# Joining the last two pairs of a convolution, and which PSUM banks their small products use

## The chip, the cores and the metric

The kernel runs on one core of a Trainium2 chip. The metric is the device time of one execution in microseconds (us). A measurement is the median of several runs.

## What is computed

Each of 64 sequences (batch) with 64 heads of 1024 positions goes through a causal long convolution, whose kernel per head is made from 64 complex exponentials (a state-space model), plus a direct term, under a length mask. The result goes through a mixture of 64 rank-16 experts with the best 16 gated by a softmax, and is added to the input:

```python
kernel = 2.0 * einsum('hn,hnl->hl', Cs, exp(dtA[:, :, None] * arange(L))).real
y = (causal_convolution(u * mask, kernel) + (u * mask) * D) * mask

scores = xf @ Wr.T
top_vals, top_idx = top_k(scores, 16)
G = zeros.at[rows, top_idx].set(softmax(top_vals))
h = einsum('nd,krd->nkr', xf, A)
out = einsum('nkr,kdr->nd', h * G[:, :, None], B) * 2.0
x = x + out
```

All data are fp32.

## The kernel before

The work is done in eight groups g of eight heads, 512 tokens each. A group has a convolution (`conv`), the gates of its tokens (`gates`, `spread_gates`) and the first expert product (`first`, which calls `seven`). After the last group come the second expert products for all groups (`second`), in the second half of the span. Tables of a group's exponentials (`tables`) are made two groups ahead.

A convolution treats its eight heads as four pairs i = 0 to 3, in blocks of 128 positions:

- `into_states(i)` (L618) turns the blocks into states: for each of two parts c, a PSUM tile pu, filled by two products that each use half of the columns of TensorE's array (shape 128*64). ScalarE copies pu to the state tile s (L623).
- `recur` (L366) lets the states decay from block to block, on VectorE, 18 small operations a pair.
- `inside(i)` (L644) opens two PSUM tiles pc, one a head, with a Toeplitz product of the block itself (shape 128*128).
- `across` (L653) adds what the states bring, with 64-row products (shape 64*128), and then multiplies pc by the mask into y on VectorE (L661). `out_of` is `inside` and `across` in one.

PSUM has eight banks, which stand in three pools: `ps_f` (four banks, tag pf) for the products h of the experts (L553), `ps_c` (two, tag pc) for pc, and `ps_k` (two, tag pk) for pu and for all small products: pb and pk in `tables` (transposed columns of the tables, L326, and kernel rows, L293), psh and psc in `gates` (scores, L722 and L731), and pg in `spread_gates` (gates transposed, L766). A tile that is opened in a bank waits until the readers of the tile before it in that bank are done. In convolution 0 alone, pairs 1 and 3 put pc into `ps_f`.

The order of the work: `conv`, `tables` and `first` are Python generators. The main loop advances them in turns: each `yield` of `conv` lets `first` issue one product of 16 matmul instructions, or as many as the yielded number says. `step(n)` inside `conv` advances the tables of a later group by n steps. Steps 1 to 8 make the sines and the tables w; steps 9 to 12 make the four columns of b and their transposes pb; the last ones make pk and the kernel rows. What is issued first is preferred, and a scheduler may then move an instruction that would wait. An fp32 product is two matmul instructions in the trace, a transpose one.

So a convolution from 1 on goes: pairs 0 and 1 into states, `recur(0, 1)`, two of `first`'s products more, pair 0 out and pair 2 in, a product, pair 1 out and pair 3 in, `recur(2, 3)`, a product, table steps, a product, pair 2 out, a product, pair 3 out, table steps. The gates of the group follow at once.

Of the kernel before, what the change touches and what calls it, by code (L numbers as in the profile page):

```python
# [37 lines left out]
F32 = mybir.dt.float32  # L38
# [6 lines left out]
P = 128  # L45
NB = 64
# [17 lines left out]
GP = HG // 2  # L64
NW = P + 1
NCH = NBLK - 1
# [26 lines left out]
def body(ctx: ExitStack, tc, x, xo, lens, par, dvec, at, bm, wt, cst, out):  # L93
# [12 lines left out]
    ps_f = ctx.enter_context(tc.tile_pool(name="ps_f", bufs=4, space=PSUM))  # L106
    ps_c = psum.enter_context(tc.tile_pool(name="ps_c", bufs=2, space=PSUM))
    ps_k = psum.enter_context(tc.tile_pool(name="ps_k", bufs=2, space=PSUM))
# [33 lines left out]
    def load_x(h):  # L142
        t = xp.tile([P, 2, NBLK * NB], F32, tag="x", name=f"x_{h}")
        nc.sync.dma_start(t, x[h : h + 2].rearrange("h p c -> p h c"))
        x_tiles[h] = t
# [57 lines left out]
    def behind_landing(t):  # L203

        tc.keep_in_program_order(G.tensor_copy(landed, t))
# [7 lines left out]
    def fourth_sum(s4, s2):  # L213

        for k in range(0, KH, 2):
            tc.keep_in_program_order(
                G.dma_start(s4[:, k : k + 2, :], at[:, KH + k : KH + k + 2, : L // 2]))
        for k in range(0, KH, 2):
            tc.keep_in_program_order(
                G.dma_start(s4[:, k : k + 2, :], s2[:, k : k + 2, :], accum_op=ALU.add))  # L220
# [144 lines left out]
    def stt(o, a, s, o1, b, o2):  # L365
        V.scalar_tensor_tensor(out=o, in0=a, scalar=s, in1=b, op0=o1, op1=o2)  # L366
        return o
# [157 lines left out]
    def masks():  # L525
        lens_f = prep.tile([P, NB], F32, tag="lensf", name="lens_f")
        V.tensor_copy(lens_f, lens_sb)
        tt(mask, feat.unsqueeze(2).to_broadcast([P, NBLK, NB]),
           lens_f.unsqueeze(1).to_broadcast([P, NBLK, NB]), ALU.is_lt)
# [65 lines left out]
    def conv(g, steps, out):  # L595
        if g == 0:
            next(steps)
        w, bt, turn, toep = tabs.pop(g)
        if g == 0:

            s_more = yp.tile([P, NBLK * TOK], F32, tag="y", name="s_more")
        y = yp.tile([P, NBLK, NS2, HH, NB], F32, tag="y", name=f"y_{g}")
        out.append(y)
        states = {}

        def into_states(i):
            h = g * HG + 2 * i
            if h not in x_tiles:
                load_x(h)
            xt = x_tiles.pop(h)  # L610
            if g == 0 and i == GP - 1:
                s = s_more[:, : 2 * NCH * NB].rearrange("p (c k b) -> p c k b", c=2, b=NB)
            else:
                s = sp.tile([P, 2, NCH, NB], F32, tag="s", name=f"s_{g}_{i}")
            for c in range(2):
                pu = ps_k.tile([P, NCH * NB], F32, tag="pk", name=f"pu_{g}_{i}_{c}")
                for hh in range(2):
                    nc.tensor.matmul(  # L618
                        pu[hh * NS : (hh + 1) * NS, :],
                        lhsT=bt[:, i, (1 - c) * P + hh * NS : (1 - c) * P + (hh + 1) * NS],  # L620
                        rhs=xt[:, hh, : NCH * NB], start=True, stop=True,
                    )
                marks["s"] = nc.scalar.copy(s[:, c], pu.rearrange("p (k b) -> p k b", b=NB))  # L623
            states[i] = xt, s

        def recur(*pairs):
            for k in range(1, NCH):
                for i in pairs:
                    s, a = states[i][1], turn[:, 0, i : i + 1]
                    stt(s[:, :, k, :], s[:, :, k - 1, :], a, ALU.mult, s[:, :, k, :], ALU.add)  # L630
                for i in pairs:
                    s, b = states[i][1], turn[:, 1, i : i + 1]
                    stt(s[:, 0, k, :], s[:, 1, k - 1, :], b, ALU.mult, s[:, 0, k, :], ALU.add)
                for i in pairs:
                    s, nb = states[i][1], turn[:, 2, i : i + 1]
                    stt(s[:, 1, k, :], s[:, 0, k - 1, :], nb, ALU.mult, s[:, 1, k, :], ALU.add)

        def inside(i):
            xt, s = states.pop(i)
            pcs = []  # L640
            for hh in range(2):
                banks, tag = (ps_f, "pf") if g == 0 and i % 2 else (ps_c, "pc")
                pc = banks.tile([P, NBLK * NB], F32, tag=tag, name=f"pc_{g}_{i}_{hh}")
                nc.tensor.matmul(pc, lhsT=toep[:, 2 * i + hh, :], rhs=xt[:, hh, :],  # L644
                                 start=True, stop=False)
                pcs.append(pc)
            return i, s, pcs

        def across(i, s, pcs, pinned=False):
            for c in range(2):  # L650
                for hh in range(2):
                    o = hh * NS
                    m = nc.tensor.matmul(  # L653
                        pcs[hh][:, NB:], lhsT=w[o : o + NS, c, i, 1:],
                        rhs=s[o : o + NS, c].rearrange("p k b -> p (k b)"),
                        start=False, stop=(c == 1),
                    )
                    if pinned:
                        tc.keep_in_program_order(m)
            for hh in range(2):  # L660
                marks["y"] = V.tensor_tensor(  # L661
                    out=y[:, :, i // 2, 2 * (i % 2) + hh, :],
                    in0=pcs[hh].rearrange("p (k b) -> p k b", b=NB), in1=mask, op=ALU.mult)

        def out_of(i):
            across(*inside(i))

        def step(n):
            for _ in range(n):
                next(steps, None)  # L670

        if g == 0:
            step(1)
        into_states(0)
        into_states(1)
        if g == 0:
            step(3)
            masks()
            first_order.close()
            step(1)  # L680
            behind_landing(toep[0:1, HG - 1, 0:1])
            fourth_sum(wa[2], wa[5])
            prep_ctx.close()
        recur(0, 1)
        if g == 0:
            into_states(2)
            into_states(3)
            first_two = inside(0), inside(1)
            across(*first_two[0], True)
            across(*first_two[1])  # L690
            recur(2, 3)
            last_two = inside(2), inside(3)
            yield
            across(*last_two[0], True)
            across(*last_two[1])
            return
        yield
        step(4)
        yield 2

        out_of(0)
        into_states(2)
        yield
        out_of(1)
        into_states(3)
        recur(2, 3)
        yield
        step(5)
        yield
        out_of(2)  # L710
        yield
        out_of(3)
        step(5)


    def gates(g, y):
# [393 lines left out]

    got = []
    steps = conv(0, steps0, got)
    next(steps)
    hp = pool(left, "hp", 1, "left")
# [7 lines left out]
    for g in range(NG):  # L1122
# [29 lines left out]
        for n in conv(g + 1, steps, got):  # L1152
            ahead(products, 1 if n is None else n)
# [40 lines left out]
    for _ in products:  # L1194
# [3 lines left out]
        if n in (5, 6):  # L1198
            i = (1, 6)[n - 5]
# [77 lines left out]
```

## Time and profile before

| | |
|---|---|
| median of three runs | 977.95 us (977.91 to 978.32) |
| the profiled execution | 978.31 us, of which the span that the profile shows is 976.5 us |
| convolution 0 | until about 50 us |
| convolutions 1 to 7 | their first states at 74.9, 137.8, 212.2, about 288.5, 364.8, 441.1 and 517.4 us |
| last score product psh | 564.3 us |
| second expert products | from about 634 us to the end |

Columns of a timeline row: start (us), length (us), engine, line, operation, out<-in, shapes, count. In brackets stands how long the engine was idle just before, and what ended that. PE is TensorE's matmuls, PEld its weight loads, DVE VectorE, ACT ScalarE. The ends of matmuls are modelled, so the distance between two starts says more than a row's length.

### The profile page before, as it was taken

How to read it: one execution, taken by the hardware profiler on the slowest of the kernel's cores; microseconds unless marked ns; L12 is line 12 of the kernel's file. 1: busy time of each engine (PE TensorE's matmuls, PEld its weight loads, DVE VectorE, ACT ScalarE, POOL GpSimd, SP SyncE). 2: the span in 40 equal slices, each digit the busy share in tenths (PEclk: the TensorE clock that was granted, in tenths of full speed). 3: DMA queues.
4: the chain of work that ended last, by engine and by line, in shares of the span. 5: the costliest groups of instructions: out<-in, count | busy, mean ns of one | idle time of the engine just before them, and what ended most of it. 6: DMA issues, size and time to landing. Idle time of an engine off the chain costs nothing.

```text
span 976.5 us, 11964 instructions
## 1 busy us (share of the span) xinstructions
PE 963.7 (99%) x4312; PEld 723.8 (74%) x4312; DVE 724.2 (74%) x1682; ACT 159.7 (16%) x310; POOL 334.8 (34%) x285
## 2 busy tenths in 40 slices
PE   7999999999999999999999999999999999999998
PEld 2476666676676686586676678888888888888887
DVE  8889798597687687686656769778966785686674
ACT  5344151230330221131101000000000000000000
POOL 0212112042023023132123112247545663754555
PEclk9999999999999999999999999999999999999999
DMA  7825234325325305315305254683674466267422
GB/s 281 226 56 167 70 119 141 108 89 155 109 75 159 114 36 158 139 55 157 140 23 167 77 178 162 198 300 105 216 260 132 168 209 231 90 214 266 134 108 108
DMA packets 67456, 143.99 MB, mean 147 GB/s; under 512 B 9478, under 2 KB 18246, under 8 KB 67398
## 3 DMA queue, kind: packets, MB, share of 16 engines
q1 hardware_dynamic: 49378, 94.40, 28.7%
q0 software_dynamic: 16864, 47.22, 15.1%
q10 hardware_dynamic: 1156, 1.61, 0.6%
q8 instruction: 34, 0.56, 0.2%
q14 instruction: 24, 0.20, 0.1%
HBM read 94.89 MB, written 47.25 MB: 146 GB/s over the span
## 4 chain that ended last, share of the span: by engine, by line
PE 93%; DVE 4%; DMA 1%; ACT 1%; issue 0%; POOL 0%; DVEq 0%
PE h L553 39%; PE s L1042 34%; PE pc L644 5%; PE pc L653 5%; PE pu L618 5%; PE psh L722 3%; PE pb L326 1%; PE pk L293 1%; DMA toep<-krows 1%; DMA krows<-ks 0%; PE last L1042 0%; PE pg L766 0%; DVE s L366 0%; PE psc L731 0%; DVE hg L355 0%
## 5 line engine op out<-in xcount | busy, mean ns | idle before, releaser
L366 DVE SCALAR_TENSOR_TENSOR s<-s,turn 128x128 f32<-128x128 f32 (+1 forms) x558 | 153.2, 321 | 26.5 <-ACT s L623 20.2
L553 PE MATMUL h<-y,waa 128*128 128x256 f32 x512 | 120.7, 383 | 0.0
L553 PE MATMUL h<-y,was 128*128 128x256 f32 x512 | 117.6, 381 | 0.0
L553 PE MATMUL h<-ty,was 128*128 128x256 f32 x512 | 116.8, 380 | 0.0
L553 PEld LDWEIGHTS h<-y,waa 128*128 128x128 f32 x512 | 94.4, 190 | 27.1 <-issue 15.3
L553 PEld LDWEIGHTS h<-y,was 128*128 128x128 f32 x512 | 96.0, 190 | 20.9 <-issue 7.2
L553 PEld LDWEIGHTS h<-ty,was 128*128 128x128 f32 x512 | 96.5, 190 | 17.5 <-issue 4.8
L804 POOL TENSOR_TENSOR hg<-h_p,gx 128x512 f32<-128x512 f32 x16 | 28.7, 1796 | 213.3 <-DVE h_p L366 210.3
L804 POOL TENSOR_TENSOR hg<-h_u,gx 128x512 f32<-128x512 f32 x32 | 48.9, 1528 | 112.1 <-DVE h_u L355 111.6
L661 DVE TENSOR_TENSOR y<-pc,mask 128x512 f32<-128x512 f32 x64 | 41.2, 684 | 44.1 <-PE pc L653 44.1
L1056 ACT COPY p<-s 128x512 f32<-128x512 f32 x28 | 16.4, 586 | 312.4 <-PE s L1042 312.4
L901 POOL TENSOR_TENSOR o<-o,acc_a 128x512 f32<-128x512 f32 x32 | 47.7, 1510 | 41.4 <-ACT acc_a L919 21.6
L644 PE MATMUL pc<-x,toep 128*128 128x512 f32 x128 | 60.0, 593 | 0.3 <-DMA toep<-krows 0.3
L553 PE MATMUL h<-ty,waa 128*128 128x256 f32 x256 | 58.6, 381 | 0.0
L777 POOL DMA_DIRECT2D gx<-gt_dram x56 | 33.6, 629 | 67.3 <-DMA gt_dram<-gt 67.3
L623 ACT COPY s<-pu 128x448 f32<-128x448 f32 x62 | 32.9, 532 | 144.3 <-PE pu L618 144.0
L618 PE MATMUL pu<-x,bt 128*64 128x448 f32 x256 | 55.1, 552 | 1.2 <-ACT gt L768 1.2
L553 PEld LDWEIGHTS h<-ty,waa 128*128 128x128 f32 x256 | 48.0, 190 | 9.9 <-issue 3.5
L653 PE MATMUL pc<-s,w 64*128 64x448 f32 x248 | 54.7, 561 | 0.0
L901 POOL TENSOR_TENSOR o<-o,b_room 128x512 f32<-128x512 f32 x32 | 49.2, 1557 | 9.8 <-DVE b_room L355 9.8
L355 DVE TENSOR_TENSOR o<-o,s 128x512 f32<-128x512 f32 x50 | 34.1, 682 | 23.0 <-PE s L1042 17.3
L355 DVE TENSOR_TENSOR hg<-hg 128x512 f32<-128x512 f32 x64 | 43.0, 684 | 9.5 <-POOL hg L804 8.8
(236 smaller groups left out, 1586.5 us busy)
## 6 DMA issues: line engine op xcount, KB each, us to landing
x<-in_x SPq DMA_DIRECT2D x32, 512.0 KB
hg_dram<-hg POOLq DMA_DIRECT2D x16, 1024.0 KB, 5.2
o<-in_xo SPq DMA_DIRECT2D x64, 256.0 KB
out<-o SPq DMA_DIRECT2D x63, 256.0 KB
gx<-gt_dram POOLq DMA_DIRECT2D x56, 256.0 KB, 6.1
qy<-hg_dram SPq DMA_DIRECT2D x28, 512.0 KB
r<-hg_dram SPq DMA_DIRECT2D x26, 512.0 KB
hg_dram<-hg POOLq DMA_DIRECT2D x16, 768.0 KB, 4.4
```

The costliest lines, as they stand in the source:

```text
L355: V.tensor_tensor(out=o, in0=a, in1=b, op=o_)
L366: V.scalar_tensor_tensor(out=o, in0=a, scalar=s, in1=b, op0=o1, op1=o2)
L553: nc.tensor.matmul(bank[:, ii, :], lhsT=fac[n - 1][:, k, (j + ii) * P : (j + ii + 1) * P], rhs=rf[n - 1][:, k, :], start=(first and ii == ...
L618: nc.tensor.matmul(pu[hh * NS : (hh + 1) * NS, :], lhsT=bt[:, i, (1 - c) * P + hh * NS : (1 - c) * P + (hh + 1) * NS], rhs=xt[:, hh, : NCH ...
L623: marks["s"] = nc.scalar.copy(s[:, c], pu.rearrange("p (k b) -> p k b", b=NB))
L644: nc.tensor.matmul(pc, lhsT=toep[:, 2 * i + hh, :], rhs=xt[:, hh, :], start=True, stop=False)
L653: m = nc.tensor.matmul(pcs[hh][:, NB:], lhsT=w[o : o + NS, c, i, 1:], rhs=s[o : o + NS, c].rearrange("p k b -> p (k b)"), start=False, sto ...
L661: marks["y"] = V.tensor_tensor(out=y[:, :, i // 2, 2 * (i % 2) + hh, :], in0=pcs[hh].rearrange("p (k b) -> p k b", b=NB), in1=mask, op=ALU ...
L777: i = queue.dma_start(gx[:, ii, :], gt_dram[g, c * n : (c + 1) * n, :].unsqueeze(1).to_broadcast([n, RANK, TOK]),)
L804: G.tensor_tensor(out=o, in0=a, in1=b, op=op)
L901: tc.keep_in_program_order(G.tensor_tensor(out=o, in0=a, in1=b, op=op_))
L1042: nc.tensor.matmul(bank[:, ii, :], lhsT=left_[i - 1][:, k, ii * P : (ii + 1) * P], rhs=right_[i - 1][:, k, :], start=(first and ii == rows ...
```

## The change

Three edits, all in `conv`, for the groups from 1 on; convolution 0 is as it was.

Pair 1's states pu are opened in the two banks of `ps_c`, not in `ps_k`, so that the states of pairs 0 and 1 have four banks together. Pair 3's tiles pc are opened in the two banks of `ps_k`, not in `ps_c`, so that pairs 2 and 3 can be open at once. And the end of the convolution is written as one stretch: `inside(2)`, `inside(3)`, then `across` for both, with both of `first`'s products ahead of it. The table steps are cut 4, 4 and 6 in place of 4, 5 and 5: none of the transposes pb is issued before the stretch.

```diff
             for c in range(2):
-                pu = ps_k.tile([P, NCH * NB], F32, tag="pk", name=f"pu_{g}_{i}_{c}")
+
+                banks, tag = (ps_c, "pc") if g and i == 1 else (ps_k, "pk")
+                pu = banks.tile([P, NCH * NB], F32, tag=tag, name=f"pu_{g}_{i}_{c}")
...
-                banks, tag = (ps_f, "pf") if g == 0 and i % 2 else (ps_c, "pc")
+                if g == 0:
+                    banks, tag = ((ps_c, "pc"), (ps_f, "pf"))[i % 2]
+                else:
+                    banks, tag = (ps_k, "pk") if i == GP - 1 else (ps_c, "pc")
...
         yield
-        step(5)
-        yield
-        out_of(2)
-        yield
-        out_of(3)
-        step(5)
+        step(4)
+        yield
+        yield
+        last_two = inside(2), inside(3)
+        across(*last_two[0])
+        across(*last_two[1])
+        step(6)
```

## The prediction

> **What bounds the kernel.** I read the page's engine row first, then TensorE's (PE's) timeline, where the start of one row minus the start of the row above is the time that a block really takes (the ends are modelled).
>
> ```profile
> PE 963.7 (99%) x4312; PEld 723.8 (74%) x4312; DVE 724.2 (74%) x1682; ACT 159.7 (16%) x310; POOL 334.8 (34%) x285
> ```
>
> PE is the bound all the way, at a granted clock of 1.00. So only two things can move the time: PE's own blocks becoming shorter, and PE idling. One steady convolution, conv 3, on PE:
>
> ```profile
> 212.20 1.72 PE L618 MATMUL pu<-x,bt 128*64 128x448 f32 x8
> 213.85 0.70 PE L553 MATMUL h<-y,waa 128*128 128x256 f32 x2
> 214.48 1.72 PE L618 MATMUL pu<-x,bt 128*64 128x448 f32 x8
> 216.13 3.29 PE L553 MATMUL h<-y,waa 128*128 128x256 f32 x14
> ...
> 243.62 0.38 PE L326 MATMUL pb<-cst_sb,b 128*128 128x128 f32 x2
> 243.84 3.62 PE L553 MATMUL h<-y,waa 128*128 128x256 f32 x16
> 247.29 1.88 PE L644 MATMUL pc<-x,toep 128*128 128x512 f32 x4
> 249.10 1.77 PE L653 MATMUL pc<-s,w 64*128 64x448 f32 x8
> 250.81 3.72 PE L553 MATMUL h<-ty,was 128*128 128x256 f32 x16
> 254.37 1.88 PE L644 MATMUL pc<-x,toep 128*128 128x512 f32 x4
> 256.18 1.77 PE L653 MATMUL pc<-s,w 64*128 64x448 f32 x8
> 257.88 0.88 PE L326 MATMUL pb<-cst_sb,b 128*128 128x128 f32 x6
> 258.60 0.60 PE L553 MATMUL h<-y,waa 128*128 128x256 f32 x2
> 259.12 1.02 PE L293 MATMUL pk<-b,cst_sb 128*2 128x256 f32 x4
> 260.08 3.65 PE L722 MATMUL psh<-y,wt_sb 128*64 128x512 f32 x16
> ```
>
> No row here idles. But blocks cost more beside a change of tile shape (the column 128*128, 64*128, 128*64). Sixteen h take 3.45 us after pb (243.84 to 247.29) and 3.56 after the 64-row products (250.81 to 254.37): 0.216 each, plus 0.10. Four Toeplitz products (pc, L644) should take 4 x 0.432 = 1.73 at the h's rate and take 1.81. Eight 64-row products (L653) run two at a time, 4 x 0.378 = 1.51, and take 1.70. So an excursion into the 64-row shape costs 0.08 + 0.19 + 0.10 = 0.37, and one into the 128*64 shape (the states' pu: 1.65 for 1.51 of work; two h between, 0.63 for 0.43) 0.34.
>
> That a joint stretch pays once is seen in conv 0, whose last two pairs already run so (chain of waits, then VectorE's timeline):
>
> ```profile
> 44.29 3.21 PE pc L653 x16
> ```
> ```profile
> 46.03 1.29 DVE L661 TENSOR_TENSOR y<-pc,mask 128x512 f32<-128x512 f32 x2 [3.24 <-PE pc L653]
> 47.53 1.29 DVE L661 TENSOR_TENSOR y<-pc,mask 128x512 f32<-128x512 f32 x2 [0.21 <-PE pc L653]
> ```
>
> Sixteen take 3.21, not 2 x 1.70. The stretch starts at 44.22 and the next block at 47.43. The first pair's multiplies start 1.80 after the stretch's start, well inside it, and the second pair's 0.10 after its end. Two multiplies take 1.29, one 0.69.
>
> **The rule on the shapes.** The Trainium skill (TensorEngine Tiling (Array Packing), Tiling Modes) says that a change of tiling mode drains TensorE; it gives no size. If a drain is the 0.10 seen after the 64-row block, two excursions fewer per conv, four changes, give 0.4 us. The rows give 0.37 + 0.34 = 0.7, because entering costs more than leaving. I use the rows.
>
> **Part A, pair 1's states in the out-of-states banks.** In the changed program's order PE issues all sixteen pu on end; the two h between them go elsewhere at 0.43. Before: 212.20 to 216.13, 3.93. After: 3.02 of work + 0.14 = 3.16, or 3.27 as the sixteen pu of conv 1 took in PE's timeline (74.92 to 78.19, with waits for copies). Gain 0.23 to 0.34; I take 0.30, and five convs (3 to 7): **1.5 us**. The banks are free: their earlier readers are multiplies some 20 us back. VectorE's recurrences start from the same copies and have about 4 us until the first product that reads them (end 223.2, product 228.0).
>
> **Part B, the tails of convs 2 to 6.** Let T be the end of the last 64-row product. Before, from the first pb to T, 243.62 to 257.88: 14.26. After: two h blocks 6.91, eight Toeplitz products 8 x 0.432 + 0.08 = 3.54, sixteen 64-row products 3.21: 13.66. Gain 0.60, part of which is only pb moved behind T.
>
> After T, pair 3's sums lie in the small products' banks, which pb needs. That is the new wait. By the conv 0 rows the four multiplies start at T - 1.41, -0.81, +0.10 and +0.70; the third ends at T + 0.79, the fourth at T + 1.39. The changed order is: two h (0.43 + 0.10, until T + 0.53), four pb (waiting for the third multiply), four pb (waiting for the fourth), two h, pk, psh. What a release costs is seen at two places:
>
> ```profile
> 562.81 1.13 PE L553 MATMUL h<-y,waa 128*128 128x256 f32 x4
> 562.91 1.29 DVE L661 TENSOR_TENSOR y<-pc,mask 128x512 f32<-128x512 f32 x2 [2.65 <-PE pc L653]
> ...
> 564.26 0.20 PEld L722 LDWEIGHTS psh<-y,wt_sb 128*64 128x64 f32 x4 [0.72 <-DVE y L661]
> ```
> ```profile
> 25.79 0.20 PEld L326 LDWEIGHTS pb<-cst_sb,b 128*128 128x128 f32 x2 [0.50 <-ACT s L623]
> ```
>
> The multiply's end at 564.20 lets PE go at 564.26. And pb's weight load waits too: at 25.79 load and product start together. The Trainium skill (TensorE: Matmul & The Clock Gate, Part 2) says that the queue pulls weight loads ahead of running matmuls; by that a load would be done when the bank comes free. The row says it isn't: 0.10 more per wait, some 1.2 us over six convs. I take the row. So the first four pb start at T + 0.87 (0.34 idle) and end at T + 1.41; the second four start at T + 1.46 and end at T + 2.00; h 0.53, pk 0.96: psh starts at T + 3.48. Before, 257.88 to 260.08 is 2.20. After holds two h more (0.43), so 3.05 compares: 0.85 lost, 0.60 won, **0.25 us lost** per conv, 1.25 in five. With the load hidden it is 0.14, with a release of 0.15 as before conv 1's psh 0.33: 0.7 to 1.65.
>
> Queued behind pb on PE are pk and psh. psh needs all four multiplies anyway, over by then. ScalarE's copies of pb, VectorE's k (waits for pk) and the sine tables come 1.3 us later after T; they have slack, since the gates' product pg comes over 20 us later in these convs. DMAs, SyncE's and POOL's orders are unchanged.
>
> **Part C, conv 7.** No tables, so no pb behind T. Before, 545.22 to 562.81 is 17.59; after, 3 x 3.45 + 0.10 + 3.54 + 3.21 = 17.21. psh waits for the same multiplies as above. Gain **0.4 us**.
>
> **Part D, conv 1's tail and the seam to conv 2**, where before PE stands:
>
> ```profile
> 123.21 3.65 PE L722 MATMUL psh<-y,wt_sb 128*64 128x512 f32 x16 [0.58 <-DVE y L661]
> ...
> 137.27 0.60 PE L766 MATMUL pg<-cst_sb,sa 128*64 128x128 f32 x4
> ...
> 140.56 0.97 PE L618 MATMUL pu<-x,bt 128*64 128x448 f32 x4 [1.16 <-ACT gt L768]
> ```
>
> Before, from T = 120.36 to the h behind the states at 143.74: 23.38, with four h (0.86) that the changed order puts elsewhere, so 22.52. After: psh at T + 3.48, psc until T + 8.46, forty h: PE is at pg at T + 17.1. Its operand comes from VectorE, whose work there is reordered: multiplies until T + 1.39, then as in the rows 123.10 to 128.89 the sums ty and f (5.8), four f and a clip (1.6), done at T + 8.8; the top-16 steps 3.8, T + 12.6. The exponential now stands behind the sine tables and a table load (1.28) on ScalarE: T + 14.3. Then w, a sum, and normalising interleaved with four b columns, about 3.3: pg at T + 17.7, 0.6 idle. pg 0.53, sixteen pu 3.17 with four banks and no wait for gt: T + 21.4. Gain 1.1, with the 0.60 before T **1.7 us**. This is the least sure sum: VectorE's chain could be 0.6 shorter, or 0.7 longer: 1.0 to 2.3.
>
> **Sum.** 1.5 - 1.25 + 0.4 + 1.7 = 2.35. The profiled execution took 978.31 (span 976.5), 0.36 above the median 977.95. 978.31 - 2.35 = 975.96, on the median's footing 975.6. The second half (from 582 us) only moves earlier. About 0.2%, 1.96 us, is what a measurement of this kernel can tell from no change; the forecast lies just past it.
>
> **Rivals.**
> - *The waits eat it.* The bank waits at their dear end (-1.65) and the seam at its poor end (1.0), pu at 0.23 x 5: 1.15 - 1.65 + 0.4 + 1.0 = 0.9, so 977.0. For it: every term is at its bound but none beyond. Against: they would have to fall so together. 25%, mostly inside 0.2%.
> - *Pair 2's multiplies wait for the joint stretch to end.* Place: VectorE's first multiply behind the stretch, in seven convs. Then all four follow T, every release is 1.2 us later (T + 2.0 and + 2.6), and psh of conv 7 too: 7 x 1.2 = 8.5 lost, 981.8, slower. It cancels the gain from a delay of 0.33 us per conv and is slower beyond doubt from 0.6. Against it stands the row at 46.03, inside the stretch; for it, that row is of conv 0 alone, where other work lay between. 7%.
> - *Waits hidden.* Load pulled ahead (-0.7), seam 2.3, pu 1.7: 3.7 won, 974.2. 5%.
> - The likeliest, 975.6 with about 1 us either way: 63%, of which four fifths are past 0.2%.
>
> Faster 0.60, same 0.33, slower 0.07. The range, 974.2 to 977.6, takes in the likeliest, both ends of the bounds and some of the first rival.
>
> **What would show it.** In the changed profile: sixteen pu in 3.2; sixteen 64-row products in 3.2 behind eight Toeplitz products; PE rows at pb with about 0.3 idle before the first four, released by VectorE's y; multiplies at T - 1.4; no wait at gt in the seam, but a short one at pg. The forecast fails if the idle at pb is over 0.7, if pg stands over 1.5 us, or if an excursion doesn't return its 0.35.

## The result and the profile after

The changed kernel takes 975.35 us (975.26 to 975.59, 9 runs), the kernel before 978.16 (977.91 to 978.33, 9 runs); the ratio is 0.9972, with a 95% interval of 0.9962 to 0.9982. The profiled execution of after took 975.34 with a span of 973.6, 2.97 below the profiled one of before. Of these 2.97, 0.17 are not the change's: after reaches conv 1's first states at 74.75, before at 74.92, and up to there the two kernels do the same (before stood 0.30 at conv 0's second Toeplitz row for a DMA, and this execution of after didn't). That leaves 2.80, and the medians are 2.81 apart.

The engine row of the page of after:

```profile
PE 961.4 (99%) x4312; PEld 726.0 (75%) x4312; DVE 725.6 (75%) x1682; ACT 160.2 (16%) x310; POOL 330.5 (34%) x285
```

The same instructions, the same bound. Conv 3 on TensorE's (PE's) timeline:

```profile
210.68 3.23 PE L620 MATMUL pu<-x,bt 128*64 128x448 f32 x16
213.84 3.72 PE L553 MATMUL h<-y,waa 128*128 128x256 f32 x16
...
241.75 3.62 PE L553 MATMUL h<-y,waa 128*128 128x256 f32 x16
245.21 3.62 PE L553 MATMUL h<-ty,was 128*128 128x256 f32 x16
248.66 3.60 PE L649 MATMUL pc<-x,toep 128*128 128x512 f32 x8
252.19 3.28 PE L658 MATMUL pc<-s,w 64*128 64x448 f32 x16
255.39 0.70 PE L553 MATMUL h<-y,waa 128*128 128x256 f32 x2
256.24 1.25 PE L326 MATMUL pb<-cst_sb,b 128*128 128x128 f32 x8
257.33 0.60 PE L553 MATMUL h<-y,waa 128*128 128x256 f32 x2
257.86 1.02 PE L293 MATMUL pk<-b,cst_sb 128*2 128x256 f32 x4
258.81 3.65 PE L728 MATMUL psh<-y,wt_sb 128*64 128x512 f32 x16
```

Sixteen states products take 3.16 (210.68 to 213.84) where two blocks and two h took 3.93. From the first h block here to the end of the 64-row products, T = 255.39, are 13.64; the same work with two transposes took 14.26. From T to psh are 3.42 with eight transposes and four h instructions, before 2.20 with six and two.

No PE row here marks the wait at pb, since the modelled end of the h row, 255.39 + 0.70 = 256.09, covers about half of it. The weight loads show it (timeline of all engines):

```profile
253.99 1.29 DVE L666 TENSOR_TENSOR y<-pc,mask 128x512 f32<-128x512 f32 x2 [4.38 <-PE pc L658]
...
255.49 1.29 DVE L666 TENSOR_TENSOR y<-pc,mask 128x512 f32<-128x512 f32 x2 [0.21 <-PE pc L658]
...
256.24 0.42 PEld L326 LDWEIGHTS pb<-cst_sb,b 128*128 128x128 f32 x4 [0.55 <-DVE y L666]
...
256.83 0.42 PEld L326 LDWEIGHTS pb<-cst_sb,b 128*128 128x128 f32 x4 [0.18 <-DVE y L666]
```

The multiplies start at T - 1.40 and T + 0.10. The third takes 0.69 and ends at 256.18, and at 256.24 the first pb goes, T + 0.85, where the two h were through at T + 0.53: 0.32 of standing. The second four wait for the fourth multiply and go at T + 1.44. In all six convs with tables the times after T are these within 0.01. The seam from conv 1 to conv 2, PE's timeline of after:

```profile
119.75 0.70 PE L553 MATMUL h<-y,waa 128*128 128x256 f32 x2
...
123.17 3.65 PE L728 MATMUL psh<-y,wt_sb 128*64 128x512 f32 x16
...
137.45 0.60 PE L772 MATMUL pg<-cst_sb,sa 128*64 128x128 f32 x4 [0.50 <-DVE sa L762]
137.98 3.28 PE L620 MATMUL pu<-x,bt 128*64 128x448 f32 x16
141.19 3.72 PE L553 MATMUL h<-y,was 128*128 128x256 f32 x16
```

The waits of 0.58 at psh and 1.16 at the states are gone, and one of 0.50 at pg is new. In conv 7, which has no tables, psh waits for y as before (PE's timeline):

```profile
559.84 1.13 PE L553 MATMUL h<-y,waa 128*128 128x256 f32 x4
561.28 3.65 PE L728 MATMUL psh<-y,wt_sb 128*64 128x512 f32 x16 [0.31 <-DVE y L666]
```

### The profile page after: what moved, and what is told of

The parts are those of the page before. It is cut to its first block, busy times and chain, and to the rows that moved or that the text cites. A ratio compares the mean times of both kernels' runs of the same rounds, so it can differ in the third digit from the quotient of the medians.

```text
span 973.6 us, 11950 instructions
## 1 busy us (share of the span) xinstructions
PE 961.4 (99%) x4312; PEld 726.0 (75%) x4312; DVE 725.6 (75%) x1682; ACT 160.2 (16%) x310; POOL 330.5 (34%) x285
## 4 chain that ended last, share of the span: by engine, by line
PE 95%; DVE 4%; issue 0%; DMA 0%; ACT 0%; DVEq 0%
PE h L553 39%; PE s L1048 34%; PE pc L649 6%; PE pc L658 5%; PE pu L620 5%; PE psh L728 3%; PE pb L326 1%; PE pk L293 1%; DVE y L666 1%; PE pg L772 0%; PE last L1048 0%; DVE ty L355 0%; PE psc L737 0%; DVE f L355 0%; DMA par_sb<-in_par 0%
## 5 line engine op out<-in xcount | busy, mean ns | idle before, releaser
L366 DVE SCALAR_TENSOR_TENSOR s<-s,turn 128x128 f32<-128x128 f32 (+1 forms) x558 | 151.1, 320 | 25.6 <-ACT s L625 20.2
L810 POOL TENSOR_TENSOR hg<-h_u,gx 128x512 f32<-128x512 f32 x32 | 46.8, 1465 | 112.3 <-DVE h_u L355 112.2
L813 POOL DMA_DIRECT2D hg_dram<-hg x32 | 25.6, 801 | 69.4 <-DVE hg L355 45.5
```

The lines of the kernel that those rows point to most:

```text
L810: G.tensor_tensor(out=o, in0=a, in1=b, op=op)
```

## The experiments

The theory: each change of array shape that goes saves its share of 0.35 us, and pb's wait for pair 3's bank gives part of it back in every conv with tables. The first rival: the joint stretch brings the gain. The second: the wait at pb costs nothing of its own, because psh stands behind it anyway. Each kernel was timed against the kernel before on the same chip (978.26 beside the first four, 978.22 beside the later ones, 978.16 beside the changed kernel).

**Each part alone.** First only the states' banks:

```diff
-                pu = ps_k.tile([P, NCH * NB], F32, tag="pk", name=f"pu_{g}_{i}_{c}")
+                banks, tag = (ps_c, "pc") if g and i == 1 else (ps_k, "pk")
+                pu = banks.tile([P, NCH * NB], F32, tag=tag, name=f"pu_{g}_{i}_{c}")
```

> Only pair 1's states in the out-of-states banks; the tails are those of before. Theory (shape changes cost, the bank wait gives part back): sixteen states products on end save 0.34 us in convs 3 to 7 (1.7) and about 0.8 in conv 2, so 2.5 won: 975.7, as good as both edits together, because the joint tails of convs 2 to 6 cost 0.17 each. Rival (the joint stretch brings the gain): about 977.5.

Measured: 976.46, ratio 0.9979 (0.9973 to 0.9985), 1.80 won. The states' 1.7 are there (212.54 to 215.70, 3.16, in conv 3). The 0.8 at conv 2 are not: there PE still waits for gt, ScalarE's copy of the gates out of pg's bank (PE's timeline of this kernel),

```profile
138.06 1.72 PE L620 MATMUL pu<-x,bt 128*64 128x448 f32 x6
140.82 2.48 PE L620 MATMUL pu<-x,bt 128*64 128x448 f32 x10 [1.04 <-ACT gt L770]
```

from T (120.62) to the h behind the states 22.61, before 22.52 for the same h. The rival is refuted: over half of the gain comes from the states alone.

Then only the stretch: pair 3 in the small products' banks, the joint tail, the steps 4, 4, 6, and the states' banks as before.

> Only the joint stretch, pair 3 in the small products' banks, table steps 4, 4, 6; the states stay in two banks. Theory: convs 2 to 6 lose 0.17 each (0.85), conv 7 wins 0.40, conv 1 and its seam win about 0.5: 978.1, no change. Rival (the stretch brings the gain): 976.3.

Measured: 977.97, ratio 0.9993 (0.9985 to 1.0001), not told from no change, as the theory had it. 1.80 and 0.29 make 2.09; both edits together won 2.81. What they win beyond the sum lies in the conv 1 seam: with the stretch alone, PE waits 0.50 for pg and then goes through the states in three pieces with h between (138.29 to 143.01, 4.72, of which 0.86 is h); with both, in one piece of 3.21.

**Taking pb's wait away.** Pair 3's 64-row products and multiplies go ahead of pair 2's, so that the small products' banks come free first:

```diff
-        across(*last_two[0])
         across(*last_two[1])
+        across(*last_two[0])
         step(6)
```

> The changed kernel, but in the joint stretch pair 3's 64-row products and multiplies come ahead of pair 2's, so that the small products' banks come free before the stretch ends. Theory (pb waits for the bank): from the stretch's end to psh 2.4 us with two h, where it is 3.42 with four: 0.58 won in convs 2 to 6, little in conv 1, where VectorE holds pg: 972.3. Rival (the wait at pb is only another one in front of psh, which needs all four multiplies): 975.3.

It was run a second time as the base of later kernels:

> Pair 3 first once more, as the base of the kernels sent with it: 971.5 on all theories.

Measured: 971.54, ratio 0.9925 (0.9909 to 0.9941), and the second time 971.81, ratio 0.9933 (0.9921 to 0.9945). That is 3.5 to 3.8 below the changed kernel, by the order of two lines. The loads and PE in conv 3 of the first run (timeline):

```profile
252.61 1.29 DVE L666 TENSOR_TENSOR y<-pc,mask 128x512 f32<-128x512 f32 x2 [4.38 <-PE pc L658]
...
254.01 1.09 PE L326 MATMUL pb<-cst_sb,b 128*128 128x128 f32 x8
254.11 1.29 DVE L666 TENSOR_TENSOR y<-pc,mask 128x512 f32<-128x512 f32 x2 [0.22 <-PE pc L658]
...
254.94 0.59 PE L553 MATMUL h<-y,waa 128*128 128x256 f32 x2
...
255.47 1.02 PE L293 MATMUL pk<-b,cst_sb 128*2 128x256 f32 x4
...
256.42 3.65 PE L728 MATMUL psh<-y,wt_sb 128*64 128x512 f32 x16
```

pb starts at T itself (254.01), and psh at T + 2.41. psh's own need, the two multiplies at 254.11, is met at 255.40, a microsecond before psh. So the second rival falls. The time is 0.5 to 0.8 below the expected one because conv 1 and its seam won too, 1.07 by the rows: pg stands at 136.53 without a wait (137.45 in the changed kernel), since VectorE got the scores a microsecond earlier.

**The same by covering it.** One product between the stretch and the tables:

```diff
         across(*last_two[0])
         across(*last_two[1])
+        yield
         step(6)
```

> The changed kernel with one more product of h (sixteen instructions) between the joint stretch and the tables' transposes. Theory (pb waits for the bank, and any work covers it): 0.54 won in convs 2 to 6, 0.5 in conv 7 where psh no longer waits for y, nothing in conv 1, whose products are used up: 972.1. Rival (tables and gates issued 3.5 us later make pg or the next states wait): 975 or more, with an idle PE at pg.

Measured: 972.59, ratio 0.9938 (0.9923 to 0.9954); as expected within 0.5. In conv 3 the product stands from T = 256.86 to 260.42, and pb follows without a wait. In conv 1 pb's wait and pg's 0.50 stand as they did, as the first expert products are used up there. (The profiled execution of this one stood 2.03 for a DMA in conv 0, so its times before conv 1 aren't compared.)

**The same by other banks.** pb goes into the out-of-states banks, with the pairs in the changed kernel's order:

```diff
-                pb = ps_k.tile([P, 1 if g == 0 else 2, 2 * P], F32, tag="pk", name=f"pb_{g}_{i}")
+                banks, tag = (ps_c, "pc") if g > 1 else (ps_k, "pk")
+                pb = banks.tile([P, 1 if g == 0 else 2, 2 * P], F32, tag=tag, name=f"pb_{g}_{i}")
```

> The changed kernel with pb in the out-of-states banks, which pair 2's multiplies free before the stretch ends; the order of the pairs is as in the changed kernel. Theory (the cost was the bank that pb waits for): as good as pair 3 first, 971.5 or 0.3 less, pb without a wait. Rival (pair 3 first won by something else in the order, not by the bank): near 975.3.

Measured: 972.66, ratio 0.9952 (0.9937 to 0.9968). The bank it was: in conv 3 psh starts at T + 1.98 (255.02 to 257.00) without any h, as pair 3 first has it with two (2.41 - 0.43). It stays 0.85 behind pair 3 first, which I hadn't expected. The seam shows why:

```profile
137.06 0.97 PE L621 MATMUL pu<-x,bt 128*64 128x448 f32 x4
138.99 2.48 PE L621 MATMUL pu<-x,bt 128*64 128x448 f32 x12 [0.95 <-ACT gt L775]
```

There the wait for the gates' copy is back, 0.95, as in before and with the states alone.

**Other standing, other excursions.** On top of pair 3 first, conv 7 gets one product between stretch and psh:

```diff
         across(*last_two[1])
         across(*last_two[0])
+        if g + 1 == NG:
+            yield
         step(6)
```

> Pair 3 first, and in conv 7, which has no tables, one product of h between the stretch and psh. Theory: the 0.6 us that PE stands before psh there goes: 971.0. Rival (the standing only moves to the last gates' product pg or behind): 971.5.

Measured: 971.10, ratio 0.9926 (0.9915 to 0.9938), 0.7 below the run of pair 3 first beside it (971.81). Only about half of that is the edit's. By the rows, from T to the first block of sixteen h behind the scores it takes 8.16 with pair 3 first (556.32 to 564.48, sixteen h between) and 11.24 here (555.88 to 567.12, thirty-two h between). Sixteen h are 3.45, so 0.37 is won. The other 0.44 of the two profiled executions stood before conv 7, where the kernels are the same. psh no longer waits:

```profile
555.88 3.72 PE L553 MATMUL h<-y,waa 128*128 128x256 f32 x16
559.54 3.65 PE L730 MATMUL psh<-y,wt_sb 128*64 128x512 f32 x16
```

And on top of that, pairs 0 and 1 are joined as well:

```diff
-        out_of(0)
-        into_states(2)
-        yield
-        out_of(1)
-        into_states(3)
+        first_two = inside(0), inside(1)
+        across(*first_two[1])
+        across(*first_two[0])
+        yield
+        into_states(2)
+        into_states(3)
         recur(2, 3)
```

with all odd pairs' states in the out-of-states banks and all odd pairs' sums in the small products' banks.

> The kernel before this one, with pairs 0 and 1 also joined: both pairs' Toeplitz and 64-row products on end, then a product of h, then the sixteen states products of pairs 2 and 3. Theory (each excursion costs 0.35): one 64-row and one states excursion fewer, 13.88 becomes 13.48 by the rows, 0.40 in each of seven convs: 2.8 less than with the product ahead of psh, 968.2. Rival (VectorE gets the states of pairs 2 and 3 together and 5 us later, and PE waits for them): no gain, with PE idle at the 64-row products.

Measured: 968.89, ratio 0.9905 (0.9892 to 0.9917), 2.2 below the one before it, the fastest kernel here. Conv 3:

```profile
222.51 3.60 PE L649 MATMUL pc<-x,toep 128*128 128x512 f32 x8
226.03 3.28 PE L658 MATMUL pc<-s,w 64*128 64x448 f32 x16
229.24 3.72 PE L553 MATMUL h<-ty,waa 128*128 128x256 f32 x16
232.89 3.23 PE L620 MATMUL pu<-x,bt 128*64 128x448 f32 x16
236.05 3.72 PE L553 MATMUL h<-y,was 128*128 128x256 f32 x16
```

From 222.51 to 236.05 are 13.54, expected 13.48: the h block between two other shapes takes 3.65. No 64-row product waits, so the rival didn't come. By the starts in the two profiled executions, convs 3 to 7 win 0.35 each, not 0.40, conv 2 0.26, and conv 1 with its seam only 0.08: there a block of h got in between the Toeplitz products, which start at 109.18 and go on at 113.88. In convs 1 and 2 VectorE's first multiplies start at T - 0.94 and T - 0.80, later than the T - 1.40 of the other convs.

## Why the prediction was right, point by point

The forecast was 975.6, with 2.35 to win; it was 975.35, with 2.81 won against a kernel before that measured 978.16 instead of 977.95. By terms, from the two profiled executions with the 0.17 before conv 1 set aside:

| | forecast | measured |
|---|---|---|
| sixteen states products on end in conv 1 | none | 0.1 (3.27 - 3.16) |
| A, the same in convs 3 to 7 | 1.5 | 1.7 (3.93 - 0.43 - 3.16 = 0.34 each) |
| B, tails of convs 2 to 6 | -1.25 | -0.85 (0.62 won, 0.79 lost each) |
| C, conv 7 | 0.4 | 0.4 (psh stands 2.98 earlier, the h block behind conv 7's states 2.58) |
| D, conv 1's tail and its seam | 1.7 | 1.4 |
| sum | 2.35 | 2.8 |

That the total came so near is partly luck: B lost 0.4 less than forecast and D won 0.3 less.

- **A** was at the upper end of its bounds: 3.16 by the sum of its work, not the 3.27 that conv 1's states took. In the kernel before, conv 1's products wait for copies in two banks (the loads' timeline of before, below). With four banks they do not, and conv 1 wins 0.11 too, which the sum had left out.

```profile
76.53 0.20 PEld L618 LDWEIGHTS pu<-x,bt 128*64 128x64 f32 x4 [0.66 <-ACT s L623]
77.28 0.20 PEld L618 LDWEIGHTS pu<-x,bt 128*64 128x64 f32 x4 [0.55 <-ACT s L623]
```

- **B**: mechanism, place and sign were right. pb was put at T + 0.87 and stood at T + 0.85, psh at T + 3.48 against 3.42. The term mis-sized was the load in front of each wait's first product. I took 0.10; the first of four transposes takes 0.16 where the next takes 0.11 (single starts 256.24, 256.40 and 256.51), so it is 0.05. All eight are through at T + 1.94, not 2.00, and 0.79 is lost, not 0.85. The row chosen against the rule on weight loads held: the first load goes when the bank is free, not earlier (256.24, load and product together).
- **C** came as forecast: 17.20 from 542.64 to 559.84, and the same 0.31 at psh as before.
- **D**: pg was forecast at T + 17.7 with 0.6 idle, and stood at T + 17.70 with 0.50 by the modelled end (0.66 by the starts). What failed is a step in front of T, "Gain 0.60", taken over from the steady convs. Conv 1 gained 0.34 there (14.26 to 13.92). With its products on end, the h block at 109.45 needs a bank that VectorE has still to read, and that read is queued behind twelve recurrence operations (DVE's timeline, then the loads', then PE's):

```profile
105.24 3.57 DVE L366 SCALAR_TENSOR_TENSOR s<-s,turn 128x128 f32<-128x128 f32 x12
108.72 0.68 DVE L366 SCALAR_TENSOR_TENSOR h_p<-h_u,h 128x512 f32<-128x512 f32 x1
```
```profile
109.45 3.32 PEld L553 LDWEIGHTS h<-y,was 128*128 128x128 f32 x16 [0.41 <-DVE h_p L366]
```
```profile
105.83 3.62 PE L553 MATMUL h<-ty,waa 128*128 128x256 f32 x16
109.45 3.72 PE L553 MATMUL h<-y,was 128*128 128x256 f32 x16
```

  The block ahead takes 3.62 from start to start where 3.45 is its work: PE stood 0.17 there, and the block itself takes 0.11 more, as its first load goes together with its product. The change had put two products on end where pair 2's sums used to lie between; I had looked at what this frees and not at what it hurries.
- **The rivals.** "The waits eat it" was at 977.0 and didn't come. "Pair 2's multiplies wait for the joint stretch to end" is refuted by the row at 253.99, 1.40 ahead of T. Its sum was wrong besides: 8.5 lost on top of 975.6 is 984.1, not 981.8. Of "waits hidden", at 974.2, the 1.7 for the states came, the hidden load and the 2.3 of the seam did not. The true alternative was none of the three: the waits at pb needn't be paid at all, as pair 3 first shows.
- **The rule on shapes.** One drain of 0.10 for each change would have made part A 0.2 a conv. The 0.34 measured agree with the rows. But the reason given, that entering costs more than leaving, does not hold for the 64-row shape when the starts are read one by one (before, conv 3). The last Toeplitz product starts at 248.58, the 64-row pairs at 249.10, 249.58, 249.96 and 250.34, the next h at 250.81, 251.13 and 251.34. Within a shape the steps are 0.43, 0.38 and 0.22. On the way in the steps are 0.52 and 0.48, on the way out 0.47 and 0.32: 0.20 too much each way. A row's start-to-start time puts the late start of the next row on the row before. The loads fit this: the load at 248.15 is ahead of its product at 248.58, but at each change the load starts with its product, and that product takes longer.

```profile
248.15 0.19 PEld L644 LDWEIGHTS pc<-x,toep 128*128 128x128 f32 x1 [0.24 <-issue]
249.10 0.30 PEld L653 LDWEIGHTS pc<-s,w 64*128 64x128 f32 x4 [0.76 <-issue]
250.81 1.38 PEld L553 LDWEIGHTS h<-ty,was 128*128 128x128 f32 x7 [0.65 <-issue]
```

  So an excursion into the 64-row shape costs 0.40, not 0.37, and the tails show it: 14.26 less 0.22 for the two transposes is 14.04, against 13.64.

Two sums of the experiments failed: the 0.8 for the states alone at conv 2, and that pb in the out-of-states banks is as good as pair 3 first. Both failed at the same place, the copy of the gates on ScalarE. Of the eight operations there that make b's columns, four stand ahead of it with the states alone (gt at 140.21) and five with pb in the other banks (138.37). With pair 3 first it goes ahead of all eight (137.36), and in the changed kernel all eight are done before pg is. Where it stands follows from the scheduler's order, which each edit moved. That this order alone is the cause was not tried by itself.

## What to carry to other kernels

Where TensorE is busy throughout, count the changes of array shape: joining blocks of one shape pays for entering and leaving once (0.34 to 0.40 us for each joining here). But a joined block holds its banks together, and whoever is next in them waits for the last reader. So let the half whose banks are wanted first come first; here the order of two lines was worth 3.5 to 3.8 us, more than the whole change. And look for such waits at the weight loads, because the modelled ends of matmuls can hide them, as with the 0.32 at pb.

## What the runs showed of the hardware

- Into the 64-row shape and out of it a change costs 0.20 each way (before, conv 3): the next product starts 0.10 late, its weight load starts with it and not ahead, and it takes 0.10 longer. Into the states' shape it is 0.14 (0.09 late and 0.05 longer: starts 214.17, 214.48 and 214.91), out of it 0.20. Sixteen 64-row products in one stretch pay the same once (3.20 or 3.21 in all kernels here).
- An h block of sixteen is 3.45 between its like, 3.56 behind another shape, and 3.65 between two other shapes. But the column of shapes alone doesn't say where a change is: ahead of pg, also 128*64, an h block takes 3.46 (208.21 to 211.67 before), and the change is paid between pg and the states.
- A weight load isn't taken ahead when its product waits for a bank: load and product start together at 256.24, 0.05 after the multiply that frees the bank ends.
